# Two graph layers on one core: centres kept in a tile of their own and copied with partitions turned, and a new table of places for the work between jobs

## The chip, the cores and the metric

The kernel runs on one NeuronCore of a Trainium2 chip. The metric is the device time of one execution in microseconds (us). Engines are named as in the profile: PE is TensorE's matmul (PEld its weight load), DVE is VectorE, ACT is ScalarE, POOL is GpSimd, SP is SyncE, which here only issues DMAs. SBUF is the on-chip memory of 128 partitions; PSUM holds matmul results in eight banks.

## What is computed

There are 128 graphs of 128 nodes with 64 features, `x` (128 x 128 x 64), and weighted adjacency matrices `adj`. Two layers, each behind a layer norm and a ReLU, are added to `x`. Cut to what matters:

```
h = max(layernorm(x), 0)
mask = adj > 0
W1a, W1b = W1[:64], W1[64:]
hid[b,j,k,:] = relu((h @ W1a)[b,j] + (h[b,j] - h[b,k]) @ W1b + b1)      # 192 wide
hm[b,j,:] = sum over k of hid[b,j,k,:] * mask[b,j,k]
x = x + hm @ W2 + deg * b2                                             # deg: row sums of mask
h = max(layernorm(x), 0)
x = x + (adj @ h) @ W.T
```

About one entry in eight of the mask is set, so the sum over neighbours goes over some 16 of 128 nodes.

## The kernel before

**Tiling.** Graphs are worked in groups of four (G = 4), 32 groups in all. Inside the ReLU stand a part that belongs to node `j` (the "centre") and a part that belongs to the neighbour `k`. `pre_proj` makes both for the nodes of a group with one projection of `h`; each is kept as two numbers that add up (the rounded value from ScalarE, `part 0`, and the remainder that VectorE subtracts, `part 1`), so that a fast fp32 form of matmul loses nothing. Before, both are stored in `ca`, one of two constant tiles, used by even and odd groups in turn: the first 448 columns of each of its four rows hold the neighbours' part, the columns `CA:CW` (384) the centres.

**Jobs.** The sum over neighbours is done slot by slot. `pre_rank` and `pre_slots` build the tile `S`: for each of four quarters of the nodes (32 partitions each) and each of D = 6 slots, a 0/1 matrix that picks the neighbour in that slot. A `Job` fills two PSUM tiles of two banks: `nodes` multiplies 32-partition pieces of `ca` by `S`, and `centres` adds the centres of the 32 nodes in question, taken from the tile `ar`, by a matmul with a 32-row identity. As PE works on the four quarters q side by side, each quarter needs the centres on its own 32 partitions. `ar[32 q .. 32 q + 31, w]` therefore holds the centres of quarter w, for each q; before, `pre_stack` makes it by 16 SBUF-to-SBUF copies on SP, one for each w and q. A job of half `jh` needs w = 2 jh and 2 jh + 1.

A group has twelve jobs, listed in `ORDER`. A job of kind 0 (eight of them, for 128 of the 192 hidden columns of one graph and one half) has 24 matmuls and is drained by VectorE with two reductions of absolute values into `hm0`. A job of kind 1 (four, for the other 64 columns of two graphs) has 32 and is drained by ScalarE with two ReLUs into `T`, which POOL then adds up into `hm1`. PSUM tiles come from a pool of three (`ps_g`), and a job takes two, so a job's first tile may be ready while its second waits for the drain of the job before. `pre_proj` takes one tile of the same pool.

**The order around the jobs.** Matmuls keep the order of the program text. On the other engines and on SP a scheduler settles the order when the kernel is built. Between the jobs stand the *pieces*: small functions for the next group (`AHEAD`), for the own one (`OWN`) and for the one before (`BEHIND`), which the tables put behind the job at that place (0 to 11). The ones that are spoken of below:

- `pre_adj` transposes the adjacency matrices and makes `maskT`; `pre_norm` is the first layer norm (VectorE's `mra`, ScalarE's `h`); `pre_rank` makes `qs`, `pre_slots` compares it into `S`; `pre_hT` transposes `h`; `pre_count` makes the counts `dn`, `ns`, `half`, `nb` from the matmuls `pd`.
- `pre_proj(g, r)` projects into `pp`, ScalarE stores two parts, then `z` and `e`, then VectorE subtracts twice; for r = 1 POOL adds `x` to `e`, which frees the tile that the next load of `x` waits for.
- `pre_edge_a` to `pre_edge_d` and `pre_place` build one-hot matrices for neighbours beyond the six slots (`et`, `R`, `qj`, `RT`, `S2`); `edge_x` uses them at the end of a group's own jobs (matmuls `px`, ScalarE's `X`), and `edge_sum` (24 matmul records `pe`, as two are seen for each fp32 product) and `edge_sum1` add what belongs to them once the group is over.
- `post0` to `post4` finish the group: output projection, the second layer norm (`mrb`, `h`), the product with `adj`, and the store.

One line a sentence can't say, the copies before:

```
for w in range(Q):
    for q in range(Q):
        sp.dma_start(d["ar"][ROWS[q], w], cas[g % 2][ROWS[w], :, :, CA:CW])
```

## Time and profile before

| | us |
|---|---|
| median of 3 runs (1621.31 to 1625.91) | 1622.84 |
| the profiled execution | 1623.33 |
| its span, first to last instruction | 1621.4 |
| PE busy (mean granted clock 0.757) | 1321.0 |
| PEld busy | 1028.0 |
| DVE busy | 826.8 |
| ACT busy | 680.2 |
| POOL busy | 588.6 |

An engine's busy time is the time in which at least one of its instructions ran. A group of rows in the profile names the output and input tiles without their numbers (`g<-id32r,ar` are the matmuls of `centres`, `g<-S,ca` those of `nodes`), how many there were, the mean of one, the idle time of the engine before them and what ended it. The granted clock is the share of TensorE's full clock that the hardware let through. Two lines of the page for the tile that is changed: the matmuls that read `ar`, and the copies that fill it (KB each, median us from issue to landing).

```profile
L182 PE MATMUL g<-id32r,ar 32*128 32x192 f32 x6144 | 379.1, 312 | 74.7 <-DMA ar<-ca 72.7
...
ar<-ca SPq DMA_DIRECT2D x512, 192.0 KB, 4.2
```

### The profile page before, as it was taken

The numbers are of one execution on the slowest core, as the hardware profiler recorded it, in microseconds if no ns is written. First come the engines' busy times: TensorE is split into PE (matmuls) and PEld (weight loads), VectorE is DVE, ScalarE is ACT, GpSimd is POOL, SyncE is SP. The second block draws the span as 40 slices with busy tenths as digits, with TensorE's granted clock in tenths as the row PEclk, the third lists the DMA queues.
The fourth block names the chain that finished last, engine by engine and source line by source line (L and its number), as shares of the span: only waits on it lengthen the run. The fifth ranks groups of instructions, "written<-read, shape, count | busy, mean of one in ns | idle before, by whom it ended". The sixth has DMA issues, their size and how long they took to land.

```text
span 1621.4 us, 33949 instructions
## 1 busy us (share of the span) xinstructions
PE 1321.0 (81%) x14023; PEld 1028.0 (63%) x14023; DVE 826.8 (51%) x1925; ACT 680.2 (42%) x1730; POOL 588.6 (36%) x748
## 2 busy tenths in 40 slices
PE   4878878778888789878788888788787888877886
PEld 2656666656666667656667666576565666665775
DVE  4455445554545455455554455555555554555543
ACT  2543345443345433444433444434444334544332
POOL 0333334333434333343333333433433343333343
PEclk7578777788768678777786667887877776777776
DMA  5224443224443224442234422344422344322330
GB/s 123 54 44 89 91 92 79 54 57 88 92 92 73 50 63 92 92 92 54 44 86 92 92 61 54 71 92 92 92 54 50 82 91 92 72 50 54 82 82 9
DMA packets 126223, 120.13 MB, mean 74 GB/s; under 512 B 43760, under 2 KB 126064, under 8 KB 126064
## 3 DMA queue, kind: packets, MB, share of 16 engines
q1 hardware_dynamic: 125312, 117.74, 33.6%
q8 instruction: 112, 1.84, 0.4%
q14 instruction: 47, 0.39, 0.1%
q10 hardware_dynamic: 752, 0.16, 0.1%
HBM read 13.01 MB, written 4.19 MB: 11 GB/s over the span
## 4 chain that ended last, share of the span: by engine, by line
SPq 27%; PE 25%; ACT 22%; DVE 10%; DMA 9%; issue 5%; POOL 2%; ACTq 0%; DVEq 0%; POOLq 0%
SPq L199 27%; PE pe L182 11%; DMA ar<-ca 9%; PE g L182 7%; ACT h L199 5%; ACT et L199 5%; ACT z L199 4%; DVE hm L199 3%; ACT T L199 3%; DVE mrb L199 3%; PE pp L182 2%; ACT ca L199 2%; ACT e L199 2%; DVE ca L199 1%; PE pd L182 1%
## 5 line engine op out<-in xcount | busy, mean ns | idle before, releaser
L199 POOL TENSOR_TENSOR T<-T 128x768 f32<-128x768 f32 (+3 forms) x512 | 475.9, 930 | 769.5 <-ACT T L199 739.4
L199 DVE TENSOR_REDUCE hm<-g 128x64 f32<-128x768 f32 x512 | 465.2, 950 | 351.3 <-PE g L182 351.3
L182 PE MATMUL g<-S,ca 32*128 32x384 f32 x4096 | 445.1, 445 | 190.6 <-DVE hm L199 88.4
L182 PEld LDWEIGHTS g<-S,ca 32*128 32x128 f32 x4096 | 242.1, 219 | 348.6 <-DVE hm L199 180.8
L182 PE MATMUL g<-id32r,ar 32*128 32x192 f32 x6144 | 379.1, 312 | 74.7 <-DMA ar<-ca 72.7
L182 PEld LDWEIGHTS g<-id32r,ar 32*128 32x128 f32 x6144 | 359.6, 230 | 101.9 <-DMA ar<-ca 100.6
L199 ACT ACTIVATE T<-g 128x768 f32<-128x768 f32 x256 | 193.1, 806 | 136.0 <-PE g L182 136.0
L199 ACT ACTIVATE hT<-ph 128x256 f32<-128x256 f32 x32 | 12.3, 383 | 312.0 <-PE ph L185 312.0
L199 DVE TENSOR_TENSOR ca<-pp,ca 128x384 fp32r<-128x384 f32 x128 | 65.4, 552 | 109.0 <-ACT e L199 109.0
L182 PE MATMUL pe<-RT,X 128*64 128x128 f32 (+1 forms) x512 | 113.0, 376 | 0.0
L182 PE MATMUL pe<-mident,z 128*64 128x128 f32 (+1 forms) x512 | 94.6, 333 | 0.0
L182 PE MATMUL pp<-wp,hT 64*128 64x448 f32 x256 | 93.9, 822 | 0.0
L199 POOL TENSOR_TENSOR hs<-hm 128x256 f32<-128x256 f32 x64 | 46.7, 730 | 123.9 <-DVE hm L199 123.9
L199 ACT ACTIVATE ca<-pp 128x384 fp32r<-128x384 f32 x128 | 55.0, 480 | 76.2 <-PE pp L182 76.1
L182 PEld LDWEIGHTS pe<-RT,X 128*64 128x64 f32 (+1 forms) x512 | 79.3, 228 | 8.6 <-issue 5.3
L182 PE MATMUL px<-ca,S 128*128 128x192 f32 x256 | 83.5, 425 | 0.0
L182 PEld LDWEIGHTS pe<-mident,z 128*64 128x64 f32 (+1 forms) x512 | 79.8, 223 | 0.0
L182 PE MATMUL pe<-maskT,ca 128*128 128x128 f32 x256 | 78.3, 403 | 0.0
L182 PE MATMUL px<-ca,R 128*128 128x192 f32 x256 | 75.6, 393 | 0.0
L182 PEld LDWEIGHTS px<-ca,S 128*128 128x128 f32 x256 | 63.4, 305 | 10.5 <-issue 9.9
L199 ACT ACTIVATE h<-x,mrb,rsb 128x64 f32<-128x64 f32 x128 | 45.9, 429 | 54.7 <-DVE mrb L199 54.7
L199 DVE TENSOR_SCALAR S<-qs 128x512 fp32r<-128x512 bf16 x192 | 67.6, 422 | 0.0
(124 smaller groups left out, 1379.2 us busy)
## 6 DMA issues: line engine op xcount, KB each, us to landing
ar<-ca SPq DMA_DIRECT2D x512, 192.0 KB, 4.2
adj<-in_adj_dram SPq DMA_DIRECT2D x32, 256.0 KB, 3.8
x<-in_x_dram SPq DMA_DIRECT2D x32, 128.0 KB, 2.2
out_dram<-ot SPq DMA_DIRECT2D x32, 128.0 KB, 3.9
w<-in_L_gnn_W_dram SPq DMA_DIRECT2D x2, 64.0 KB, 3.2
bias<-in_L_gnn_b_dram ACTq DMA_DIRECT2D x2, 32.0 KB, 2.8
w<-in_L_gnn_W_dram SPq DMA_DIRECT2D x2, 32.0 KB, 2.4
w2a<-in_L_gnn_W_dram ACTq DMA_DIRECT2D x1, 32.0 KB, 2.3
```

The lines of the kernel that those rows point to most:

```text
L182: return tc.keep_in_program_order(nc.tensor.matmul(*args, **kw))
L199: ins = f(*args, **kw)
```

## The change

Three things are changed.

- The centres no longer go through `ca`. `ar` is taken from its pool in `pre_proj` of r = 0, and ScalarE and VectorE store the centres into `ar[:, 0]`. `ca` becomes narrower (448 columns for 832), and `edge_x` reads the centres from `ar[:, 0]`.
- `pre_stack` copies `ar[:, 0]` into `ar[:, 1]`, `ar[:, 2]` and `ar[:, 3]`, turned by 32, 64 and 96 partitions, each in two copies (96 + 32, 64 + 64 and 32 + 96 rows). The centres of quarter w now stand for quarter q at `ar[.., (w - q) mod 4]`, and `centres` reads them there.
- `ORDER`, `AHEAD`, `OWN` and `BEHIND` are written anew: the jobs of one half `jh` come together, most pieces move to other places, and `edge_sum` is cut into two halves of two graphs each.

```diff
-    CA = 2 * H + C1
-    CW = CA + 2 * H
+    CW = 2 * H + C1
+    AW = 2 * H
@@ ca_of
-            a = CA + p * H if t else p * (H + C1)
-            return cas[g % 2][:, part, r, a + us.start : a + us.stop]
+            c = groups[g]["ar"][:, 0, part, r] if t else cas[g % 2][:, part, r]
+            a = p * H if t else p * (H + C1)
+            return c[:, a + us.start : a + us.stop]
@@ pre_proj
             if r == 0:
+                d["ar"] = grp.tile([P, Q, 2, 2, AW], F32R, tag="ar", name=f"ar{g}")
...
             def part(i, t):
-                c = cas[g % 2][:, i, r]
-                c = c[:, CA:CW] if t else c[:, 0 : 2 * (H + C1)]
-                return c.rearrange("n (p u) -> n p u", p=2)[:, :, 0:H]
+                if t:
+                    return d["ar"][:, 0, i, r].rearrange("n (p u) -> n p u", p=2)
...
@@ pre_stack
-            d = groups[g]
-            d["ar"] = grp.tile([P, Q, 2, 2, 2 * H], F32R, tag="ar", name=f"ar{g}")
-            for w in range(Q):
-                for q in range(Q):
-                    sp.dma_start(
-                        d["ar"][ROWS[q], w].bitcast(F32),
-                        cas[g % 2][ROWS[w], :, :, CA:CW].bitcast(F32),
-                    )
+            a = groups[g]["ar"].bitcast(F32)
+            for k in range(1, Q):
+                m = k * QN
+                sp.dma_start(a[0 : P - m, k], a[m:P, 0])
+                sp.dma_start(a[P - m : P, k], a[0:m, 0])
@@ edge_sum
-        def edge_sum(g):
+        def edge_sum(g, p):
...
-            for b in range(G):
+            for b in range(2 * p, 2 * p + 2):
...
+            if p == 0:
+                return
@@ Job.centres
-                    groups[g]["ar"][ROWS[q], 2 * self.jh + v, part, r, a : a + P],
+                    groups[g]["ar"][ROWS[q], (2 * self.jh + v - q) % Q, part, r, a : a + P],
@@ the tables
         AHEAD = {
             0: (pre_adj,),
-            1: (pre_norm, pre_hT, pre_rank),
-            2: (lambda g: pre_slots(g, 0, 3), pre_count),
-            3: (lambda g: pre_slots(g, 3, D), lambda g: pre_proj(g, 0),),
-            4: (pre_edge_a,),
-            6: (lambda g: pre_proj(g, 1), pre_stack),
-            9: (pre_edge_b, pre_place),
-            10: (pre_edge_c,),
-            11: (pre_edge_d,),
+            1: (pre_rank, pre_norm),
+            2: (pre_hT, lambda g: pre_slots(g, 0, 3)),
+            3: (pre_count, lambda g: pre_slots(g, 3, D)),
+            4: (lambda g: pre_proj(g, 0),),
+            5: (lambda g: pre_proj(g, 1), pre_stack),
+            6: (pre_edge_a,),
+            7: (pre_place, pre_edge_b),
+            8: (pre_edge_c,),
+            9: (pre_edge_d,),
         }
         OWN = {
-            7: (lambda g: edge_x(g, 0),),
-            8: (lambda g: edge_x(g, 1),),
+            10: (lambda g: edge_x(g, 0),),
+            11: (lambda g: edge_x(g, 1),),
         }
         BEHIND = {
-            0: (slot_sum,),
-            1: (edge_sum,),
+            0: (slot_sum, lambda g: edge_sum(g, 0)),
+            1: (lambda g: edge_sum(g, 1),),
             2: (edge_sum1,),
-            4: (post0,),
-            5: (post1,),
-            7: (post2,),
-            8: (post3,),
+            6: (post0,),
+            7: (post1, post2),
+            9: (post3,),
             10: (post4,),
         }
         ORDER = []
         for r in range(2):
-            for s in range(2):
-                ORDER += [(0, 2 * s + r, 0), (0, 2 * s + r, 1), (1, r, s)]
+            for jh in range(2):
+                ORDER += [(0, r, jh), (1, r, jh), (0, 2 + r, jh)]
```

A job in `ORDER` is (kind, graph or pair, half).

More of the change, by code (lines that the diff above doesn't have):

```diff
@@ L559, in part @@
             def part(i, t):
-                c = cas[g % 2][:, i, r]
-                c = c[:, CA:CW] if t else c[:, 0 : 2 * (H + C1)]
-                return c.rearrange("n (p u) -> n p u", p=2)[:, :, 0:H]
+                if t:
+                    return d["ar"][:, 0, i, r].rearrange("n (p u) -> n p u", p=2)
+                ends = [cas[g % 2][:, i, r, p * (H + C1) : p * (H + C1) + H] for p in range(2)]
+                a = ends[0]
+                return bass.AP(
+                    tensor=a.tensor, offset=a.offset,
+                    ap=[list(a.ap[0]), [ends[1].offset - a.offset, 2], [1, H]],
+                )
             for t in range(2):
@@ L689, in slot_sum @@
                 )
-        def edge_sum(g):
+        def edge_sum(g, p):
             d = groups[g]
-            ph = mtile(f"pe0{g}")
-            for b in range(G):
+            if p == 0:
+                d["pe0"] = mtile(f"pe0{g}")
+            ph = d["pe0"]
+            for b in range(2 * p, 2 * p + 2):
                 o = ph[:, b * N : (b + 1) * N]
@@ L703, in edge_sum @@
                     )
+            if p == 0:
+                return
             d["u0"] = tmp.tile([P, G, N], F32, tag="u0", name=f"u0{g}", bufs=1)
```

## The prediction

> **What bounds the kernel now.** I read the waits first, TensorE's own rows, because PE is the busiest engine (1321.0 us, 81%) and its remaining 300 us are waits.

> ```profile
> PE g L182 <- DVE hm L199: 88.4, 123, 2.3
> PE g L182 <- ACT T L199: 85.2, 33, 2.8
> PE g L182 <- DMA ar<-ca: 72.7, 112, 2.8
> PE pq L182 <- ACT hT L199: 14.7, 31, 0.5
> ```

> Columns: total us, times, longest. Three waits of like size: for PSUM buffers that VectorE (`hm`) and ScalarE (`T`) have not drained, and for copied centres. No queue but PE is near full, so what counts is where these fall. The chain that ended last names the copies first:

> ```profile
> SPq 27%; PE 25%; ACT 22%; DVE 10%; DMA 9%; issue 5%; POOL 2%; ACTq 0%; DVEq 0%; POOLq 0%
> SPq L199 27%; PE pe L182 11%; DMA ar<-ca 9%; PE g L182 7%; ACT h L199 5%; ACT et L199 5%; ACT z L199 4%; DVE hm L199 3%; ACT T L199 3%; DVE mrb L199 3%; PE pp L182 2%; ACT ca L199 2%; ACT e L199 2%; DVE ca L199 1%; PE pd L182 1%
> ```

> So the loop from one group to the next closes over SP issuing 16 copies, their landing, then PE `pe` (`edge_sum`). Its pieces of 24 `pe` matmuls, listed in order of time, come once a group; from the one at 139.21 us to that at 1521.22 us lie 28 groups, 49.4 us each. A group has 12 places, 4.1 us a place. In one group the timeline (start, length, what, idle before) shows:

> ```profile
> 728.35 0.73 PE L182 MATMUL g<-id32r,ar 32*128 32x192 f32 x5 [1.01 <-DMA ar<-ca]
> 728.92 1.82 DVE L199 TENSOR_REDUCE hm<-g 128x64 f32<-128x768 f32 x2 [5.23 <-PE g L182]
> ...
> 749.25 1.01 PE L182 MATMUL g<-S,ca 32*128 32x384 f32 x6 [2.81 <-ACT T L199]
> ...
> 754.86 0.69 PE L182 MATMUL g<-S,ca 32*128 32x384 f32 x2 [1.79 <-DVE hm L199]
> ...
> 758.78 14.73 SPq L199 DMA_DIRECT2D ar<-ca  x16
> ```

> The copies start at 758.78 and the next group's second job waits for the last ones. Last, stretches of that group, for the granted clock (after PE, PEld, DVE, ACT and POOL busy):

> ```profile
> 723.77:726.77 3.00, 1.53 (x8) 0.83 (x8) 0.00 (x0) 0.00 (x0) 1.94 (x4) 0.91 0.93 192
> 726.77:729.77 3.00, 1.95 (x9) 1.53 (x10) 0.84 (x1) 0.00 (x0) 0.00 (x0) 0.50 0.61 148
> 729.77:732.77 3.00, 3.00 (x17) 3.00 (x15) 0.98 (x2) 0.00 (x0) 0.00 (x0) 0.50 0.00 0
> 735.77:744.77 9.00, 7.93 (x119) 5.62 (x116) 7.16 (x18) 4.10 (x11) 4.05 (x5) 1.00 0.00 0
> 747.00:757.00 10.00, 5.78 (x50) 3.79 (x52) 4.93 (x20) 7.70 (x23) 4.02 (x5) 0.50 0.00 1
> 757.00:766.00 9.00, 9.00 (x80) 7.98 (x80) 2.75 (x4) 3.48 (x10) 3.83 (x4) 0.50 0.68 142
> ```

> The clock is 1.00 or 0.50. Twice a group it falls, after the wait for copies and after the two buffer waits at 747 to 755; it rises only after PE has been busy without a gap. So a wait also makes the work behind it take twice as long.

> **The change, part by part.** I count per group and multiply by 31 boundaries.

> *Fewer, larger copies, one place earlier.* 16 copies of 128 rows of 1,536 bytes (3.15 MB) become six with 384 rows of 6,144 bytes (2.36 MB). ScalarE and VectorE store 128x384 as before (480 and 552 ns), into `ar`, and `edge_x` reads `ar`: nothing added. Six issues stand in SP behind the same `x` load (0.37 us), whose wait, POOL's `e` (0.73 us), runs beside the subtraction that the copies need anyway. Now the last `ca` subtraction ends at 758.5 and the last copy lands 19.2 us later (772.49 + 5.24). With three quarters of the bytes at the rate of now, 14.73 x 0.75 = 11.0, plus 4.2 to land, 15.2 us. At best it is six issues at 0.59 (the shortest `ar` issue) and the least landing, 2.7: 6.2 us; at worst long rows move at half the rate: 26 us. I take 15.2, the row of the same path. The first job now needs the last copy, where before it needed the first eight, but the subtraction lies some six places ahead: 24.7 us, with 9 to spare; those six jobs hide it. Gone: 72.7 less 8.4 in the first 62 us, 64.3 / 31 = **-2.1**. Should the cover go, this comes back, and every us past it in full. A store into `ar` must wait for readers two groups back, done over 4 places (16 us) before.

> [...]

> *The clock at the boundary.* The 31 pieces of 24 `pe` matmuls last 4.9 us on average, mostly at 0.50. At 1.00 they take half, 2.45. The halves of `edge_sum` now follow the first and second job, behind place 11's `edge_x`, with no wait for copies: I take **-2.3**; ends 0 and -2.45. `edge_x` (`px`, 16 matmuls, two blocks of 1.95 us as the starts 757.46 and 761.83 and the jobs after them show) has a median of 415 ns against a least of 268, so it runs at 0.50 nearly always. At places 10 and 11 it comes after PE has been busy a while; two thirds of one block: **-1.3**; ends 0 and -1.95. This work lies on PE in its program order, which is the path here.

> *New: compares ahead of a VectorE drain.* `pre_slots(.., 0, 3)` and `(.., 3, D)` are emitted at places 2 and 3, and in the order built all six `S` compares (2.10 us) stand on VectorE ahead of the drain of place 2, a kind-0 job, where before the job beside them was kind 1, drained by ScalarE. Place 3's job waits for it, and behind it on PE all else. From the end of `pq` (735.04) to the last compare (738.02) is 3.0 us; with half of a drain (0.95) 4.0. PE has the job (1.0 at full clock), `edge_sum1` (1.02) and `pre_hT` (0.46) meanwhile and a little of the next job: **+1.4**. Ends 0 (at half clock the cover is 5.0) and 2.7 (no cover but the job and a little).

> *New: the two projections next to each other* (places 4 and 5). `pp` of r = 1 takes the one PSUM buffer that `pp` of r = 0 holds until `ca`, `z`, `e` and the subtractions are done: 0.87 + 1.04 + 0.56 + 1.02 + 0.2 of hand-over = 3.7 us. Cover is one kind-0 job, 1.74 at half clock (764.83 to 766.57): 1.96 of wait, for the 0.42 + 0.31 + 0.33 = 1.06 that PE now waits around that projection (740.96, 743.55, 744.32): **+0.9**; ends -1.06 and 1.6.

> *The norms' chain.* The drain of place 8's job stands on VectorE behind `mrb`, `rsa`, `mra`, and these behind ScalarE's `h`, as the 1.79 shows today. There `pp` covered 2.1 us (750.99 to 753.07); now `prt` alone, 0.6: **+1.5**, ends 0 and 2.1. The wait for `T` behind `et` and `R` stays (85.2 / 32 = 2.66), but `pj` (0.95) now runs in it: **-0.95**; ends -2.66 and 0.

> Idle: -2.1 + 1.4 + 0.9 + 1.5 - 0.95 = +0.75. Clock: -3.6. Net -2.85 us x 31 = -88: a span of 1533.0 for 1621.4. That execution took 1623.33 with what lies around the span, 0.5 over the median of 1622.84, so 1534 on the median's scale.

> [...]

> **Rivals.** *The clock does not come back at the boundary.* The waits at places 3, 5 and 8 spread over the group, and no stretch is full enough to raise it before `edge_sum` and `edge_x`. Then the -3.6 is gone and +0.75 x 31 = +23 is left: 1645. It decides once under 0.75 of the 3.6 arrives. If the stretch 735.77 to 744.77 also ran at half, 7.93 of work would become 15.9, up to 6.9 more a group. For it: four waits where now there are three. Against it: after 757 nine full us raise the clock today, and places 9 to 11 keep such a stretch.

> *The waits shrink too.* The 88.4 and 85.2 come where PE runs a long block and the drain engines then queue up (VectorE idle 5.23 before 728.92). With pieces spread evenly half of it, 87 us, could go as well: 1447. Against: the same chains in the same order on ScalarE.

> *The copies are no earlier where it counts.* If long rows run at half the rate (26 us) the first job waits where the second did: about 1620. Against: fewer bytes at every rate seen.

> **How the numbers follow.** My forecast has 0.67 (own range 1480 to 1595), the shrinking waits 0.16, the clock rival 0.13, slow copies 0.04. About 0.3% (5 us) is what a measurement of this kernel can tell from no change. Faster: 0.67 + 0.16 and a little of the last, 0.84; within 0.3%: 0.04; slower 0.12. The range 1450 to 1610 leaves out the ends of both.

> **What would show it.** PE's wait for `ar` near 0 after the first 60 us; pieces of 12 `pe` at about 1.3 us; `px` median under 415 ns; PE waits for `hm` above 88.4 and for `T` below 85.2; the group near 46.5 us. I am wrong if the `pe` pieces still run at half clock, or if PE waits for `ar`.

## The result and the profile after

| | before | after |
|---|---|---|
| median, us | 1622.07 (4 runs, 1619.2 to 1625.91) | 1685.95 (4 runs, 1684.66 to 1686.83) |
| span of the profiled execution | 1621.4 | 1685.1 |
| PE busy / not busy in it | 1321.0 / 300.4 | 1330.1 / 355.0 |
| mean granted clock | 0.757 | 0.705 |

The ratio is 1.0392, interval 1.0368 to 1.0415: slower by 64 us, where 88 us less were forecast. A group takes 51.5 us for 49.5 (means over 22 groups; most of after's take 51.2). A median leaves out executions over 1.5% longer than the fastest of the same kernel; there are such only in e4 below (three of ten) and e13 (one of four).

First TensorE's waits in the trace of after (columns as before: total us, times, longest), and the matmuls that read `ar`, from the page's groups.

```profile
PE g L182 <- DVE hm L199: 199.1, 66, 3.6
PE pp L182 <- DVE ar L199: 70.2, 31, 2.5
PE g L182 <- ACT T L199: 31.8, 32, 2.4
PE pq L182 <- DVE maskT L199: 17.8, 30, 0.6
PE g L182 <- DMA ar<-ar: 11.8, 1, 11.8
```

```profile
L182 PE MATMUL g<-id32r,ar 32*128 32x192 f32 x6144 | 353.5, 335 | 11.8 <-DMA ar<-ar 11.8
```

The wait for copies is gone but for one at the start. The waits for `hm` have become half as many and more than twice as long in sum: over 3 us each where they were 0.7. A wait of 2.3 us a group for the projection's buffer is new. The chain that ended last no longer has SP's queue in it; VectorE's compares `S`, which it did not name before, now hold 7%:

```profile
PE 49%; ACT 23%; DVE 22%; issue 4%; DMA 1%; SPq 0%; ACTq 0%; DVEq 0%
PE g L182 24%; DVE hm L199 7%; DVE S L199 7%; ACT T L199 7%; PE px L182 6%; PE pp L182 5%; ACT et L199 5%; PE pe L182 5%; ACT z L199 3%; ACT h L199 2%; PE pga L182 2%; PE pd L182 2%; DVE ar L199 2%; PE pgq L182 2%; PE po L182 2%
```

One group of after in the timeline (start, length, what, idle before). All four long waits of TensorE are in it, and the copies:

```profile
708.44 4.55 POOL L199 TENSOR_TENSOR T<-T 128x768 f32<-128x768 f32 x4 [4.40 <-ACT T L199]
710.53 3.54 DVE L199 TENSOR_SCALAR S<-qs 128x512 fp32r<-128x512 bf16 x6
714.99 1.01 PE L182 MATMUL g<-S,ca 32*128 32x384 f32 x6 [2.92 <-DVE hm L199]
725.27 1.87 PE L182 MATMUL pp<-wp,hT 64*128 64x448 f32 x4 [2.29 <-DVE ar L199]
736.49 0.62 PE L182 MATMUL g<-S,ca 32*128 32x384 f32 x6 [0.86 <-ACT T L199]
742.10 1.01 PE L182 MATMUL g<-S,ca 32*128 32x384 f32 x6 [3.55 <-DVE hm L199]
```

```profile
730.92 6.47 SPq L199 DMA_DIRECT2D ar<-ar  x6
```

The first two rows are the surprise. The six compares, 2.10 us before, take 3.54, and they lie beside POOL's additions. Over the whole trace a compare costs 651 ns for 422 before:

```profile
L199 DVE TENSOR_SCALAR S<-qs 128x512 fp32r<-128x512 bf16 x192 | 112.4, 651 | 0.0
```

Last the stretches of the same group at one clock each (length, then PE, PEld, DVE, ACT and POOL busy, then the granted clock):

```profile
700.77:714.42 13.65, 10.71 (x157) 9.06 (x153) 9.09 (x14) 3.64 (x7) 7.67 (x10) 1.00 0.13 31
714.42:721.25 6.83, 6.26 (x66) 5.49 (x68) 3.90 (x9) 0.88 (x2) 0.00 (x0) 0.50 0.00 0
721.25:724.66 3.41, 1.73 (x30) 1.06 (x25) 0.56 (x2) 2.82 (x9) 2.62 (x2) 1.00 0.00 0
724.66:734.90 10.24, 9.63 (x77) 6.77 (x77) 5.31 (x10) 4.95 (x17) 2.14 (x5) 0.50 0.35 90
734.90:738.31 3.41, 2.55 (x33) 1.76 (x30) 2.03 (x17) 2.88 (x6) 1.09 (x1) 1.00 1.02 226
738.31:751.97 13.66, 10.11 (x88) 8.86 (x90) 5.97 (x11) 5.98 (x15) 5.47 (x8) 0.50 0.25 62
```

The boundary (703 to 708, where `edge_sum` is) runs at 1.00, as forecast. But the clock falls three times a group where it fell twice, and 30.7 of the 51.2 us are at 0.50. Two of the falls come in the midst of long waits (the 2.92 us that end at 714.99, the 2.29 that end at 725.27). The third, at 738.31, comes a little ahead of the longest wait, behind a stretch whose only wait is the 0.86 us for `T`.

### The profile page after: what moved, and what is told of

It reads as the page before. It is cut to its first block, busy times and chain, and to the rows that moved or that the text cites. A ratio compares the mean times of both kernels' runs of the same rounds, so it can differ in the third digit from the quotient of the medians.

```text
span 1685.1 us, 33624 instructions
## 1 busy us (share of the span) xinstructions
PE 1330.1 (79%) x14023; PEld 1069.4 (63%) x14023; DVE 865.6 (51%) x1925; ACT 678.4 (40%) x1730; POOL 608.7 (36%) x748
## 4 chain that ended last, share of the span: by engine, by line
PE 49%; ACT 23%; DVE 22%; issue 4%; DMA 1%; SPq 0%; ACTq 0%; DVEq 0%
PE g L182 24%; DVE hm L199 7%; DVE S L199 7%; ACT T L199 7%; PE px L182 6%; PE pp L182 5%; ACT et L199 5%; PE pe L182 5%; ACT z L199 3%; ACT h L199 2%; PE pga L182 2%; PE pd L182 2%; DVE ar L199 2%; PE pgq L182 2%; PE po L182 2%
## 5 line engine op out<-in xcount | busy, mean ns | idle before, releaser
L199 POOL TENSOR_TENSOR T<-T 128x768 f32<-128x768 f32 (+3 forms) x512 | 494.5, 966 | 796.5 <-ACT T L199 766.4
L182 PE MATMUL g<-S,ca 32*128 32x384 f32 x4096 | 461.8, 502 | 235.9 <-DVE hm L199 199.1
L199 DVE TENSOR_REDUCE hm<-g 128x64 f32<-128x768 f32 x512 | 465.0, 949 | 110.9 <-PE g L182 110.9
L182 PEld LDWEIGHTS g<-S,ca 32*128 32x128 f32 x4096 | 267.8, 259 | 357.7 <-DVE hm L199 252.6
L182 PEld LDWEIGHTS g<-id32r,ar 32*128 32x128 f32 x6144 | 372.2, 263 | 12.2 <-DMA ar<-ar 12.2
L182 PE MATMUL g<-id32r,ar 32*128 32x192 f32 x6144 | 353.5, 335 | 11.8 <-DMA ar<-ar 11.8
L199 ACT ACTIVATE T<-g 128x768 f32<-128x768 f32 x256 | 192.9, 805 | 401.9 <-PE g L182 401.9
L199 DVE TENSOR_TENSOR ca<-pp,ca 128x384 fp32r<-128x384 f32 x64 | 35.7, 557 | 252.2 <-ACT e L199 250.4
L182 PE MATMUL pp<-wp,hT 64*128 64x448 f32 x256 | 108.5, 943 | 70.2 <-DVE ar L199 70.2
L199 DVE TENSOR_SCALAR S<-qs 128x512 fp32r<-128x512 bf16 x192 | 112.4, 651 | 0.0
L199 POOL TENSOR_TENSOR hs<-hm 128x256 f32<-128x256 f32 x64 | 46.4, 725 | 128.7 <-DVE hm L199 126.8
L199 DVE TENSOR_TENSOR ot<-po,x 128x256 f32<-128x256 f32 x32 | 13.6, 425 | 144.7 <-PE po L182 144.7
L182 PEld LDWEIGHTS pp<-wp,hT 64*128 64x128 f32 x256 | 32.7, 303 | 80.5 <-issue 80.4
L182 PE MATMUL pe<-RT,X 128*64 128x128 f32 (+1 forms) x512 | 83.2, 306 | 0.0
L199 ACT ACTIVATE X<-px 128x256 f32<-128x256 f32 (+1 forms) x128 | 35.3, 328 | 105.0 <-PE px L182 105.0
L199 ACT ACTIVATE ca<-pp 128x384 fp32r<-128x384 f32 x64 | 31.5, 492 | 108.5 <-PE pp L182 108.1
L182 PE MATMUL px<-ca,S 128*128 128x192 f32 x256 | 73.5, 380 | 0.0
L182 PE MATMUL pe<-mident,z 128*64 128x128 f32 (+1 forms) x512 | 70.9, 278 | 0.0
L199 POOL TENSOR_TENSOR e<-e,x 128x256 f32<-128x256 f32 x32 | 23.3, 728 | 125.0 <-ACT e L199 125.0
L182 PE MATMUL px<-ar,R 128*128 128x192 f32 x256 | 67.1, 355 | 0.0
L199 ACT ACTIVATE z<-pp,ns 128x128 f32<-128x128 f32 (+1 forms) x256 | 66.5, 358 | 0.0
L199 DVE TENSOR_SCALAR maskT<-adjT 128x512 fp32r<-128x512 f32 x32 | 13.6, 426 | 98.4 <-ACT T L199 54.9
```

Of the source, the lines that this page charges most:

```text
L182: return tc.keep_in_program_order(nc.tensor.matmul(*args, **kw))
L199: ins = f(*args, **kw)
```

## The experiments

In every table "idle" is the span less PE's busy time, and "group" is the mean time from one group's `maskT` to the next over 22 groups, taken from the timeline.

### Copies or table?

e1 keeps the new storing and the six copies and puts back the old order of jobs, the old tables and the whole `edge_sum`; e2 is its complement, the new order and tables with the sixteen copies.

```diff
 # e1, against the changed kernel (e2: the same lines the other way, on the kernel before)
-        def edge_sum(g, p):
+        def edge_sum(g):
-            1: (pre_rank, pre_norm),
-            2: (pre_hT, lambda g: pre_slots(g, 0, 3)),
+            1: (pre_norm, pre_hT, pre_rank),
+            2: (lambda g: pre_slots(g, 0, 3), pre_count),
...
-            for jh in range(2):
-                ORDER += [(0, r, jh), (1, r, jh), (0, 2 + r, jh)]
+            for s in range(2):
+                ORDER += [(0, 2 * s + r, 0), (0, 2 * s + r, 1), (1, r, s)]
```

> The copies and the narrow ca of the changed kernel, with the job order, the tables and the whole edge_sum of the kernel before. Order theory (the new table of places costs, the copies gain): the wait for ar nearly goes (64 us of 72.7 lie behind the first group), and with it part of the half clock at the boundary, so 1490 to 1580 us. Copy theory (large copies or their writes slow the engines): about 1686 us, and the wait for ar is no smaller than 70 us.

> The kernel before with the new job order, tables and halved edge_sum, but with its 16 copies out of ca. Order theory: no better than the changed kernel, 1680 to 1720 us, with waits for hm near 199 us and S compares near 650 ns. Copy theory: near the kernel before, 1600 to 1640 us.

Measured: e1 1474.29 us, ratio 0.9108 (0.9042 to 0.9174); e2 1684.16 us, ratio 1.0378 (1.0328 to 1.0428). The waits of e1:

```profile
PE g L182 <- DVE hm L199: 89.7, 125, 2.3
PE g L182 <- ACT T L199: 85.3, 33, 2.8
PE g L182 <- DMA ar<-ar: 28.7, 18, 11.8
```

The copies alone take 148 us off, and PE's busy time falls from 1321.0 to 1214.4 with the same 14,023 matmuls: 41 us of idle time went, and 107 us of the half clock behind it (granted clock 0.794 for 0.757). Both theories had expected less than that of them. e2 came out as its order theory had it (waits for `hm` of 200.6 us, compares of 651 ns). The table costs 212 us on top of the copies (1474 to 1686), and with the table in place the copies bring nothing (1684 and 1686): the sixteen old ones, issued a place earlier, make PE wait for only 6.3 us there. So the whole loss is the table's.

### POOL's additions and the compares

e3 leaves out four of the five additions that POOL makes for each ScalarE job of the changed kernel; e4 has them and fixes the compares' place on VectorE, three behind the drain of place 2 and three behind the counts; e7 is e3's edit on e1.

```diff
 # e3 on the changed kernel, e7 on e1
-                n = D // 2
-                for m in (2 * D, D, n):
-                    pool.tensor_tensor(t[:, 0:m], t[:, 0:m], t[:, m : 2 * m], ALU.add)
-                pool.tensor_tensor(t[:, 0], t[:, 0], t[:, 1], ALU.add)
 # e4
-                vec.tensor_scalar(
+                cmp = vec.tensor_scalar(
...
+                tc.keep_in_program_order(cmp)
```

> The changed kernel with four of the five additions on POOL behind each kind-1 job left out (hm1 is then the sum of two of the 24 slot terms). Theory that POOL's additions slow VectorE's compares where both run: the S compares fall from a mean of 651 to about 420 ns, the wait for hm at place 3 falls by 1.4 us a group, 1630 to 1650 us. Rival, that the compares are slow for another reason (the copies, the place after a mask): they stay near 650 ns and the time near 1686.

> The changed kernel with the S compares kept in program order on VectorE: three behind the drain of place 2, three behind the counts of place 3, instead of six ahead of the drain. Theory that the compares ahead of the drain are the main loss: the 2.92 us wait of PE at place 3 goes, the clock stays at 1.00 past it, 1560 to 1630 us. Rival, that the waits at places 5, 8 and 9 set the time: 1660 to 1690 us.

> The kernel with the copies alone changed, without four of the five additions that POOL makes for each ScalarE-drained job (left out: hm of these jobs is the sum of two of its 24 terms). Theory (VectorE's compares and two-operand steps are slowed only while POOL adds; in the old table few of them fall beside the additions, mainly mrb with 1412 ns): the compares stay near 420 ns, mrb falls to about 150 ns, and the time falls by 20 to 60 us from 1474, to 1415 to 1455; against the 180 us that the same omission took off the changed kernel, the additions then account for most of the difference between the two tables. Rival (POOL's additions cost the same in either table, through the release of T): the time falls by 120 to 200 us, to 1275 to 1355.

| | time, us | ratio to before | compare, ns | `mrb`, ns | PE busy / idle |
|---|---|---|---|---|---|
| before | | | 422 | 1412 | 1321.0 / 300.4 |
| after | 1685.95 | 1.0392 | 651 | 952 | 1330.1 / 355.0 |
| e3 | 1505.34 | 0.9275 (0.9232 to 0.9319) | 424 | 148 | 1210.4 / 295.7 |
| e4 | 1629.9 | 1.0033 (0.9986 to 1.008) | 440 | 952 | |
| e1 | 1474.29 | 0.9108 | 424 | 1412 | 1214.4 / 259.8 |
| e7 | 1445.69 | 0.8909 (0.8885 to 0.8934) | 441 | 148 | 1230.5 / 206.4 |

Without the additions both VectorE steps have their short times, so it is POOL that stretches them. In the trace of after, 157 of the 192 compares overlap an addition and take 704 ns, the other 35 take 414. The same omission is worth 181 us in the new table and 29 in the old, as e7's first theory had it. But e4 took only 56 us off, which is the upper end of the range that was expected: the compares then cost 440 ns, they stand on VectorE where they were meant to, and the time is still that of the kernel before. And e3 took off far more than was expected of it. Of its 181 us, 120 are PE's busy time: clock (0.787 for 0.705), not waits. e3 also shortens `mrb`, which e4 leaves at 952 ns; how its 181 us divide between the two was not tried.

### The table in parts

e5 puts the new order of jobs on e1. e9, e10, e11 and e13 each add one part of the table to e5, e14 adds two.

```diff
 # e5, on e1
-            for s in range(2):
-                ORDER += [(0, 2 * s + r, 0), (0, 2 * s + r, 1), (1, r, s)]
+            for jh in range(2):
+                ORDER += [(0, r, jh), (1, r, jh), (0, 2 + r, jh)]
 # e9, on e5: places 1 to 3
+            1: (pre_rank, pre_norm),
+            2: (pre_hT, lambda g: pre_slots(g, 0, 3)),
+            3: (pre_count, lambda g: pre_slots(g, 3, D), lambda g: pre_proj(g, 0)),
 # e10, on e5
+            4: (lambda g: pre_proj(g, 0),),
+            5: (lambda g: pre_proj(g, 1), pre_stack),
+            6: (pre_edge_a,),
 # e11, on e5
+            6: (post0,),
+            7: (post1, post2),
+            9: (post3,),
 # e13, on e5: edge_sum(g, 0) at 0 and edge_sum(g, 1) at 1, edge_x at 10 and 11, and
+            7: (pre_place, pre_edge_b),
+            8: (pre_edge_c,),
+            9: (pre_edge_d,),
 # e14: e9 and e10 together
```

> The kernel with the copies alone changed (1474 us), and on top of it only the new order of the twelve jobs (kinds 0,1,0 by column half instead of 0,0,1); the places of the other steps and the undivided edge sum stay as they were. Theory (the six compares cost 651 instead of 424 ns each where they fall beside POOL's additions of a ScalarE-drained job, and which job they fall beside is set by the order of jobs as well as by the table): the order alone puts a ScalarE-drained job at place 1 and its additions beside the compares of places 2 and 3; the mean compare is then well over 500 ns, TensorE's wait for hm is over 130 us, and the time is 1540 to 1640. Rival (the table of steps is at fault, the compares standing ahead of the drain that the next job needs; the order of jobs is harmless): the compares stay near 424 ns and the time within 1460 to 1500.

> The kernel with the copies and the order of jobs changed (1466 us, e5), and on top of it only the early part of the new table: the rank ahead of the norm, hT at place 2, the counts at place 3. Theory (the early part brings the compares onto the chain of the next job, 2.9 us a group where e5 has 1.24, and with it the half clock): the wait for hm after the compares is over 2.5 us a group and the time rises by 40 to 110 us, to 1505 to 1575. Rival (each place's wait is absorbed by the others; no part alone does it): within 1450 to 1490.

> The kernel of e5, and on top of it only the middle part of the new table: the projections at places 4 and 5 and the edge step behind them at place 6. Theory (the adjacent projections put a wait of about 2 us a group on TensorE at pp): a wait for ar at pp of 50 to 75 us in all; the wait of 3.7 us that e5 has behind its second projection, for hm, goes or stays by the norms, which are not moved. The time rises by 20 to 80 us, to 1485 to 1545. Rival (moving the second projection away from the norms' step takes away that 3.7 us wait, which weighs more): faster than 1460.

> The kernel of e5, and on top of it only the steps behind the jobs moved: post0 from place 4 to 6, post1 and post2 to 7, post3 to 9; the edge sum stays whole. Theory (the chain of the norms, h, mrb, rsa, mra, stands ahead of a drain that the next job waits for, 3.55 us a group in the changed kernel, whatever place it has, and e5 pays 3.7 us for it already): no more than 30 us either way, 1440 to 1495. Rival (at the later places it has no cover, and the time rises by more than 50 us): 1515 or more.

> The kernel of e5, and on top of it only the edge part of the new table: the edge steps at places 7 to 9, edge_x at 10 and 11, the edge sum in two halves. My own prediction's term (the clock at the boundary and under edge_x, -2.3 and -1.3 us a group) expects px under 350 ns and the time down by 40 to 110 us, to 1355 to 1425. Theory of the remaining loss (the dense blocks moved together leave the places 2 to 9 without filling work, so that every wait there is bare): up by 30 to 100 us, 1495 to 1565. Within 1450 to 1485 neither is shown, and the loss comes of the parts meeting.

> The kernel of e5 with the early and the middle part of the new table together (e9 and e10 in one). Theory (the parts add): 1466 + 6 + 119, 1575 to 1605. Rival (they meet: with the first projection away from place 3, the late counts and the compares fall beside POOL's additions, 651 ns a compare where e9 and e10 have 464): over 1630, compares over 600 ns.

| | time, us | against e5 | PE busy / idle | group, us | compare, ns |
|---|---|---|---|---|---|
| e5 | 1466.16 (0.8995 to 0.905 of before) | | 1207.0 / 258.5 | 44.4 | 464 |
| e9 early | 1471.75 (0.9053 to 0.9123) | +6 | 1194.2 / 273.4 | 44.5 | 464 |
| e10 projections | 1585.45 (0.9743 to 0.9824) | +119 | 1304.2 / 279.9 | 48.1 | 463 |
| e11 post | 1461.9 (0.899 to 0.9061) | -4 | 1181.6 / 277.1 | 44.4 | 463 |
| e13 edge | 1496.43 (0.9192 to 0.9298) | +30 | 1151.4 / 327.9 | 44.7 | 651 |
| e14 early and projections | 1574.92 (0.9654 to 0.9745) | +109 | 1299.6 / 273.8 | 47.7 | 463 |
| after: all of them | 1685.95 | +220 | 1330.1 / 355.0 | 51.5 | 651 |

Four readings. The order of jobs does no harm, nor do the early part and the steps behind the jobs: the theories of e5 and e9 fell, and e11's stood. The middle part (both projections, with `pre_edge_a` moved behind them) is the largest single one, larger than e10's theory had it, and its loss is not the wait that it puts on TensorE: idle rises by 21 us, busy by 97 (granted clock 0.737 for 0.799). Which of its moves costs that was not separated. In e10's timeline:

```profile
730.05 1.02 PE L182 MATMUL pp<-wp,hT 64*128 64x448 f32 x4 [2.10 <-DVE ar L199]
734.70 0.68 PE L182 MATMUL g<-S,ca 32*128 32x384 f32 x2 [1.23 <-DVE rsa L199]
735.83 1.65 PE L182 MATMUL g<-S,ca 32*128 32x384 f32 x14 [0.45 <-DVE hm L199]
```

The 14 matmuls at 735.83 take 1.65 us, where 14 take 0.97 in e5 (706.02). In the trace of after 16 of them take 1.66 us at 0.50 (717.81) and 0.98 at 1.00 (705.35), so those of e10 ran at half the clock. e14 came out as if the two parts added (its theory had 1575 to 1605), with compares of 463 ns. Third, the edge part does what the prediction said of it and pays for it elsewhere: `px` falls to 302 and 280 ns and busy by 56 us, and idle rises by 69, of which 61 are a wait for copies (2.77 us where a group begins). Its trace is of its fastest execution, 1480.97 us, so the two add up to 14 us and not to 30; the time is at the lower end of what its second theory expected. Fourth, that part, and not the moved counts, is what puts the compares under POOL's additions. POOL and the compares in e5, then in e13:

```profile
709.01 4.29 POOL L199 TENSOR_TENSOR T<-T 128x768 f32<-128x768 f32 x4 [1.71 <-ACT T L199]
...
712.72 2.34 DVE L199 TENSOR_SCALAR S<-qs 128x512 fp32r<-128x512 bf16 x6
```

```profile
714.13 4.55 POOL L199 TENSOR_TENSOR T<-T 128x768 f32<-128x768 f32 x4 [7.56 <-ACT T L199]
...
716.21 3.54 DVE L199 TENSOR_SCALAR S<-qs 128x512 fp32r<-128x512 bf16 x6
```

With the whole edge sum behind the second job (kind 1), PE is busy with it while POOL adds, and `pq` and the compares come 3.7 us after the additions began; with half of it they come 2.1 us after, in their midst.

The parts add up to 151 (6 + 119 - 4 + 30), not to 220. Three kernels took one step back from the changed one: e6 moves the second projection one place away, e15 puts the whole middle part back, e17 the whole edge sum.

```diff
 # e6
-            5: (lambda g: pre_proj(g, 1), pre_stack),
-            6: (pre_edge_a,),
+            6: (lambda g: pre_proj(g, 1), pre_stack, pre_edge_a),
 # e15
+            3: (pre_count, lambda g: pre_slots(g, 3, D), lambda g: pre_proj(g, 0)),
+            4: (pre_edge_a,),
+            6: (lambda g: pre_proj(g, 1), pre_stack),
 # e17
+            0: (slot_sum,),
+            1: (edge_sum,),
```

> The changed kernel with the second projection and the stacking moved from place 5 to place 6, one job further from the first. Theory (each wait of the group costs by itself, and the adjacent projections' wait of 2.29 us a group, 70 us in all, is one of them): TensorE's wait for ar at pp falls to under 20 us and the time to 1610 to 1650. Rival (the group is held at a whole number of clock windows by the compares, the norms and the half clock, so that a wait removed at one place is found again at the next): the pp wait falls, those of g rise by about as much, and the time stays within 1670 to 1700.

> The changed kernel with the middle part alone put back: projections at places 3 and 6, the edge step at 4. Theory (the adjacent projections are the first cause in the changed kernel too): the wait at pp goes (70 us), the time falls by 80 us or more, to 1500 to 1600. Rival (the compares and the norms hold the group at fifteen clock windows whatever the projections do, as e6 suggests, where moving them by one place made it worse): 1640 to 1720.

> The changed kernel with the edge sum alone put back in one piece of 24 matmuls behind the second job. Theory (the halving moved 12 of the matmuls away from between the first ScalarE-drained job and the slots, so that the compares start 2.1 us after POOL's additions instead of 3.7 us; and the group falls back by whole clock windows): the compares cost under 500 ns, and the group comes to 47.8 us, one window less, 1560 to 1600. Rival (the norms and the projections hold fifteen windows by themselves): compares under 500 ns, but 1640 to 1690.

| | time, us | ratio to before | PE busy / idle | group, us | compare, ns |
|---|---|---|---|---|---|
| e6 | 1762.48 | 1.0885 (1.0831 to 1.0938) | 1379.4 / 381.3 | 54.6 | 651 |
| e15 | 1662.56 | 1.0232 (1.0179 to 1.0286) | 1339.5 / 330.1 | 51.4 | 651 |
| e17 | 1674.62 | 1.0299 (1.0225 to 1.0373) | 1310.0 / 364.6 | 51.0 | 461 |

In all three the thing that was taken away went (no wait at `pp` in e6 and e15, compares of 461 ns in e17), and the waits came back at other places. e6 got 77 us slower, outside both of its ranges, and the rivals of e15 and e17 stood: taking one cause away from the slow kernel is worth 23 and 11 us, where putting one alone into the fast kernel costs up to 119.

### The clock by itself

If the half clock is the larger part of the loss, work in the waits should bring it back, even work that nobody reads. e8 adds 33 such matmuls a group to the changed kernel; e12, e16 and e18 try it on the faster ones.

```diff
 # e8, on the changed kernel
+        def filler(g, n):
+            f = mtile(f"fill{g}_{n}")
+            for _ in range(n):
+                mm(f, oneb, S_fill, start=True, stop=True)
...
-            2: (pre_hT, lambda g: pre_slots(g, 0, 3)),
+            2: (pre_hT, lambda g: pre_slots(g, 0, 3), lambda g: filler(g, 10)),
-            5: (lambda g: pre_proj(g, 1), pre_stack),
+            5: (lambda g: filler(g, 9), lambda g: pre_proj(g, 1), pre_stack),
-            8: (pre_edge_c,),
+            8: (pre_edge_c, lambda g: filler(g, 14)),
 # e12, on e5
+            6: (lambda g: pre_proj(g, 1), pre_stack, lambda g: filler(g, 15)),
 # e16, on e11
+            5: (lambda g: pre_proj(g, 1), pre_stack, lambda g: filler(g, 10)),
 # e18, on e16
+            8: (lambda g: filler(g, 12),),
```

> The changed kernel with 33 further matmuls a group that nobody reads (a constant bf16 tile, 128 x 512), put on TensorE where it waits: 10 after the slots of place 2, 9 ahead of the second projection, 14 after place 8. They add 33 x 0.21 to 0.43 us, 7 to 14 us a group, to TensorE's work. Theory (half of the loss is the half clock that several short waits bring, so that work in the waits raises the clock): the granted clock rises from 0.705 to 0.85 or more, the matmuls of the jobs come to 1.00 and the time falls to 1560 to 1650 in spite of the added work. Rival (the clock follows other things, or the drains set the time): clock under 0.80, time 1690 to 1900.

> The kernel of e5 with 15 unread matmuls a group (bf16, 128 x 512) behind the second projection, ahead of its longest wait (3.7 us for hm, after which TensorE runs at half the clock for some 12 us). They add 3.2 us a group at full clock, 6.4 at half, in a wait that is there anyway. Theory (a wait of over 3 us costs its length and half the clock for the jobs behind it): the clock rises from 0.80 to 0.87 or more and the time falls by 40 to 130 us, to 1335 to 1425. Rival (the clock is lost at the next wait instead, or the work overfills the wait): 1450 to 1520.

> The kernel of e11 with the second projection at place 5 and 10 unread matmuls a group behind it. Theory (e12 had its clock at 0.90 and lost the gain to a wait for the copies, 106 us, as its subtractions ended too late for the next group's first job; one place earlier is enough): the wait for the copies falls to under 20 us and the time to 1330 to 1430. Rival (the second projection nearer to the first brings back the wait at pp): 1450 to 1560.

> The kernel of e16 with 12 further unread matmuls a group behind place 8, ahead of its longest wait (2.9 us for hm behind the norms). Theory (that wait is what halves the clock once a group): the clock goes over 0.90, the group leaves 44.4 us, and the time falls to 1340 to 1430. Rival (VectorE's and ScalarE's chains take 44 us a group whatever the clock): 1445 to 1475.

| | time, us | ratio to before | granted clock | group, us |
|---|---|---|---|---|
| e8 | 1504.37 | 0.9273 (0.9229 to 0.9317) | 0.909 | 45.5 |
| e12 | 1466.82 | 0.9045 (0.9009 to 0.908) | 0.900 | 44.5 |
| e16 | 1457.85 | 0.8982 (0.8941 to 0.9024) | 0.842 | 44.4 |
| e18 | 1366.43 | 0.8432 (0.8371 to 0.8492) | 0.933 | 41.2 |

e8 is the clearest experiment of the study: more work, 182 us less time, better even than expected. Its waits, the added matmuls and its compares:

```profile
PE g L182 <- ACT T L199: 64.8, 51, 2.4
PE g L182 <- DVE ar L199: 25.3, 31, 1.8
PE pq L182 <- DVE maskT L199: 17.7, 30, 0.6
PE g L182 <- DVE hm L199: 16.9, 38, 2.3
```

```profile
L182 PE MATMUL fill<-sfill,oneb 128*128 128x512 bf16 x930 | 276.6, 442 | 29.7 <-ACT hT L199 14.2
L199 DVE TENSOR_SCALAR S<-qs 128x512 fp32r<-128x512 bf16 x192 | 112.5, 652 | 0.0
```

The compares are as slow as in the changed kernel and the table is the same; what differs is the work in the waits and the clock. The added matmuls (930 of 1023 have a record) are busy for 277 of PE's 1298.4 us (eight at 712.87 take 3.38, 0.42 each; ten in e18 at 720.19 take 2.33, 0.23 each), so the kernel's own take some 1020 where they took 1330. Idle time falls from 355 to 207 us, by less than was added: the gain is in the clock.

e12 and e16 show that filling one wait is not enough; both came out in the range of their rival, though not for its reason. e12 has its clock at 0.90 and gains nothing, since PE then waits 106 us for copies that are issued behind a projection at place 6; e16 has that one place earlier, and still its longest wait, 2.9 us behind the norms. e18 fills this one too, as its theory had it, and is the fastest kernel of the study, 260 us under the kernel before beside which it ran (1626.15). Its line of busy times:

```profile
PE 1185.1 (87%) x14705; PEld 861.2 (63%) x14705; DVE 804.3 (59%) x1926; ACT 675.7 (50%) x1730; POOL 602.0 (44%) x748
```

PE is busy for 145 us less than in the changed kernel, with 682 matmuls more. Which combination of places would reach this clock without unread work was not tried.

## Why the prediction was wrong, point by point

Per group (a 31st): span +2.06, forecast -2.85, an error of 4.9. Idle +1.76 for +0.75, so 1.0 of the error; PE's busy time +0.29 for -3.6, so 3.9 of it. **The step that failed is the clock: I priced it where it was to be gained (-2.3 and -1.3) and left it as it was everywhere else, though I had just booked three new waits there.** The clock is 1.00 or 0.50, so by its means (0.757 and 0.705) 0.49 of the span was at half clock before and 0.59 after. The reading under it was loose too: in the group that I took, the clock falls at 746.7, 0.3 us into the wait for `T`, and not after the two buffer waits. Nor does half the clock make the work take twice as long: 1.7 times for the 16 matmuls above (0.98 and 1.66 us).

- *Copies, -2.1.* The wait went as forecast, 72.7 us to 11.8, though the new table does that without larger copies (e2, 6.3 us). From the first issue to the last landing are some 13 us (6.47 of issues and 6.5), where 15.2 were taken. Long rows don't move at half the rate here: in 736.50 to 742.10 the turned copies move 217 GB/s with the DMA engines 0.92 busy, and the sixteen of before 208 at 0.95 in 766 to 772. e1 shows that the copies alone would have been a gain of 148 us, clock included, where my terms for the copies and the clock together came to 5.7 a group (177).
- *The clock at the boundary, -2.3, and under `px`, -1.3.* The first came, or most of it: the `pe` records sum to 209.4 us for 285.9, -2.5 a group, and the time in which any of them runs falls from 194.1 to 139.7, -1.8; but e1 has 227.0 with the sum undivided, so most of it came with the copies. The second came by half (`px` 140.6 for 159.1, -0.6; its median is still 415 ns). What was not seen is the other side. `py` rose from 43.3 to 73.0 us, `pp` from 116.6 to 132.1, `pgq` from 21.6 to 35.3, `pd`, `po`, `pga` and `pty` by 37.3 together: 96 us of records (they overlap, so not all of it is time), in the stretches at 0.50 behind the new waits.
- *Compares ahead of a drain, +1.4.* The wait is there and is 2.92, beyond the end of 2.7. Two sizes were off: the compares took 3.54 us, as they lay beside POOL's additions, where I had them from a trace in which they did not; and that comes from the halved edge sum (e13; undone in e17, 461 ns), which I had costed as a pure gain. The early part, with the moved counts, costs 6 us by itself (e9).
- *Adjacent projections, +0.9.* The wait was sized well (1.96 forecast, 2.29 found; idle +0.7 a group in e10). Its price was not: the middle part of the table costs 119 us alone, 3.8 a group, 3.1 of it PE's busy time.
- *The norms' chain, +1.5.* The wait went from 1.79 to 3.55, +1.8. Moved alone the steps cost nothing (e11), but e5, from which e11 starts, already has a wait of 3.7 there.
- *T, -0.95.* It gave -1.7 (85.2 to 31.8 us).
- *The rivals.* "The clock does not come back at the boundary" (0.13) came nearest, with 1645, and had the sign right and the clock as the cause, but the place wrong: the boundary got its clock and the middle lost it. Its clause on a further stretch at half clock came nearest to what happened, and I gave it a price but no share of the chances. I had argued against it from a stretch that raises the clock today, not from the stretches behind the new waits.

## What to carry to other kernels

On this kernel a wait on TensorE had two prices, its length and the half clock of the work behind it, and the second was the larger (e10: 0.7 us more of idle time a group and 3.1 more of busy time). So price a table of places by where the clock is lost as well as by where waits go, and try the parts of it one at a time, for here they did not add (151 us for 220). A step that is "only" moved changes which engines run at the same time: look for the pairs that slow each other, as POOL's additions did the compares here (704 ns for 414).

## What the runs showed of the hardware

**POOL and VectorE.** The compares (one bf16 input, rounded fp32 output, 128 x 512) take 414 ns alone and 704 beside POOL's additions (35 and 157 of the 192 in after); `mrb`, four columns wide, takes 148 ns without them and 952 or 1412 with them (e3, after, before). The additions are longer as well: four take 4.55 us beside the compares of after, and 3.97 at 738.09 in the kernel before, where none are beside them. Why they slow each other, no run shows.

**The group's period comes in steps.** The mean periods of many of the kernels lie near 41.2, 44.4, 47.7, 51.2 and 54.6 us: e18 at 41.2, e5, e11 and e16 at 44.4, e14 at 47.7, the median of after at 51.2, e6 at 54.6 (there two groups, 56.8 and 52.4, in turn). Divided by 12, 13, 14, 15 and 16 they give 3.41 to 3.43 us. From the trace of after, the first instruction that tells one group from the next:

```profile
708.35 0.43 DVE L199 TENSOR_SCALAR maskT<-adjT 128x512 fp32r<-128x512 f32 x1 [3.08 <-PE pe L182]
759.53 0.43 DVE L199 TENSOR_SCALAR maskT<-adjT 128x512 fp32r<-128x512 f32 x1 [3.06 <-ACT T L199]
```

That is the step of the grid; the expectations call it a clock window. Where single groups lie between the steps, several together may not: three of e3 take 136.5 us, 40 steps, and seven of e4 355.0 us, 104 steps. A group that is shortened by less than a step then seems to fall back into place, with its waits elsewhere, which would be why e6, e15 and e17 gained so little. That is argued from the periods, not shown: the kernel before, e1, e8, e12 and e13 have no such repeat.
